# Eight PSUM banks as a ring of pairs and a ring of single banks, and a new order of fc1, fc2 and the chunks' bursts

## The chip, the cores and the metric

The kernel runs on one core of one Trainium2 chip. The metric is the device time of one execution in microseconds; the kernel before takes 4109.72 us (median of three runs, 4108.55 to 4111.58). Five engines work beside each other: TensorE (PE; its weight loads are shown apart as PEld), VectorE (DVE), ScalarE (ACT), GpSimd (POOL) and SyncE (SP), which here only starts transfers. Matmuls write to PSUM, which has 8 banks of 512 fp32 values in each of 128 partitions. A bank can be written again only when ACT or DVE has read ("evicted") what is in it.

## What is computed

The reference normalizes an image of 8 channels, sends it through a small Fourier network and adds the result to the image; then it adds a 3 x 3 dilation of the normalized sum. There are 8 images of 256 x 256. Cut to what matters:

```python
x = x + fno(gn(x))                      # 8 images, 4 groups of 2 channels
x = x + dilate_3x3(gn(x))               # max over 3x3, border -2

def fno(x):                             # each group has WID = 10 channels inside
    h = gconv1x1(concat(x, grid), fc0)
    for i in range(4):                  # the four "layers"
        h1 = irfft2(mix(rfft2(h)))      # 24 x 12 modes are mixed, the rest is zero
        h2 = gconv1x1(h, w[i])
        h = h1 + h2
        if i < 3: h = gswish(h, beta[i])
    h = gswish(gconv1x1(h, fc1), beta[3])   # 10 -> 128 channels in each group
    return gconv1x1(h, fc2)                 # 128 -> 2
```

All arithmetic is fp32.

## The kernel before

An image's rows lie in 11 chunks. For each layer the kernel computes, chunk by chunk:

- the **burst** (tile `p_z`): h1 + h2 of a chunk in four banks, 16 small matmuls for the 1x1 convolution (32 x 32 tiles of the PE array) and 8 for the inverse transform along a row (32 x 128 tiles); ACT evicts it with Silu;
- the **turn**: DVE transposes the chunk's new h in blocks of 32 x 32 into one of three slots of `turned`;
- for each two chunks the **transform** along the row (`p_d`, four banks) and the **gather** (`p_u`, one bank), whose copy is what the next layer's spectrum reads.

Between layers come the spectrum across the rows (`p_at`, `p_b`), the mixing of modes on DVE (`mix`, `p_f`) and the tables for the next bursts (`p_g`). The last two convolutions of an image, its **head**, are 128 steps: **fc1** (`p_fc` at L627, four banks, 32 x 128 tiles, ACT evicts with Silu) and, for every two steps, **fc2** (`p_fc` at L649, one bank, 128 x 32 tiles, DVE adds it to y). The head of image b is interleaved with the layers of image b + 1, and the dilation of the image before with both, as generators that are stepped:

```python
def ps_z(name):                                    # all of PSUM: four pairs of banks
    return ps.tile([128, 2, 512], F32, tag="z", bufs=4, name=name)
def ps_a(name):
    return ps_z(name)[:, 0, :]

def copy(i, dst, src):                             # alone: no head runs (image 0)
    if alone[0] and i % 2: nc.scalar.activation(dst, src, AF.Identity)
    else:                  nc.vector.tensor_copy(dst, src)
def copy_2(i, dst, src):
    if i % 2: nc.scalar.activation(dst, src, AF.Identity)      # L199
    else:     nc.vector.tensor_copy(dst, src)                  # L201

# spectrum across the rows: eight transposes into a pair
    t = ps_z(f"p_at_{b}_{l}_{j0}")                             # L320, copied at L195
# tables for the bursts, two channels in a pair
    p = ps_z(f"p_g_{b}_{l}_{o}")                               # L404 / L409, copied at L195
# ... (cut)

def turn(c):                                                   # L430, two DVE transposes
    ...
def transform(k):
    pair = [ps_z(f"p_d_{b}_{l}_{k}_{i}") for i in range(2)]
    for v in range(8):
        for q in range(NQ):
            mm(pair[q // 2][part(v % 4), q % 2, : 240 * n], fw8[part(q), v, :], t[...], ...)   # L447
    for i in range(2):
        copy_2(i, e[:, 2 * i : 2 * i + 2], pair[i][:, :, : 240 * n])
def gather(k):
    p = ps_a(f"p_u_{b}_{l}_{k}")
    ...                                                        # L461, copied at L464 / L467
def burst(c):
    pair = [ps_z(f"p_z_{b}_{l}_{c}_{i}") for i in range(2)]
    ...                                                        # L476 / L479, then L482
    for i in range(2):
        dst = h[:, c, 2 * i : 2 * i + 2, :]
        if l < 3: nc.scalar.activation(dst, pair[i], AF.Silu)                  # L488
        else:     nc.scalar.activation(dst, pair[i], AF.Identity, bias=bias3)  # L490

# one layer; "yield (n,)" asks for exactly n head steps, a plain number for a share of them,
# "even" / "odd" for one step more if the count of steps is not so
        if l == 3:
            yield "odd"
            for c in range(NCH):
                burst(c)
                ...                                # side work: the next image's first spectrum
                yield (LAST,)                      # LAST = 2
            return
        yield "even"
        for c in range(NCH):
            k = c // 2
            if c % 2 == 0:
                burst(c)
                yield (1,)
                turn(c)
                if k > 0: transform(k - 1)
            else:
                burst(c)
                if k > 0: gather(k - 1)
                yield (1,)
                turn(c)
        out_["sw"] = [load_sw(l + 1, 0), load_sw(l + 1, 1)]
        yield 1
        gather(k - 1)
        transform(k)
        yield 2
        gather(k)
        yield 1

# the head
        def first(n):
            pair = [ps_z(f"p_fc1_{b}_{n}_{i}") for i in range(2)]
            for g in range(G):
                mm(pair[g // 2][:, g % 2, :], w1[part(g), blk, :], hs[k][part(g), :], ...)     # L627
            for i in range(2):
                nc.scalar.activation(act[:, 2 * i : 2 * i + 2, :], pair[i], AF.Silu)           # L629
        def second(n):
            y, acc = box["y"], ps_a(f"p_fc2_{b}_{n}")
            ...                                                # L649: steps n and n + 1; added at L654
        for n in range(STEPS):
            if n % 2 == 0 and n > 3: second(n - 4)
            first(n)
            yield
        second(STEPS - 4)
        second(STEPS - 2)
```

PE, DVE and ACT each run their instructions in the order in which they are written here. A tile of a tag takes the place of the tile of that tag that many allocations (`bufs`) earlier, and waits for its last reader.

Of the kernel before, what the change touches and what calls it, by code (L numbers as in the profile page):

```python
# [10 lines left out]
F32 = mybir.dt.float32  # L11
AF = mybir.ActivationFunctionType
# [6 lines left out]
HW = 256  # L19
# [13 lines left out]
NBLK = 3  # L33
NCH = 11
NQ = 4
CS = 2 * NCH
PIX = 2 * HW
DR = 2
STEPS = 128
LAST = 2  # L40
SIDE = 4.2


# [1 line left out]
def fno_dilate_kernel(ctx: ExitStack, tc: tile.TileContext, a: dict, out: bass.AP):  # L45
    nc = tc.nc
    mm = nc.tensor.matmul
# [4 lines left out]
    ps = ctx.enter_context(tc.tile_pool(name="ps", bufs=2, space=PSUM))  # L52
# [1 line left out]


    def ps_z(name):
        return ps.tile([128, 2, 512], F32, tag="z", bufs=4, name=name)

    def ps_a(name):
        return ps_z(name)[:, 0, :]  # L60

    def part(i):
        return slice(32 * i, 32 * i + 32)
# [23 lines left out]
    fw8 = load("fw8", (128, 8, 32), nc.sync)  # L87
# [14 lines left out]
    bias3 = load("bias3", (128, 1))  # L102
    w1 = load("w1", (128, NBLK, HID))
# [4 lines left out]
    h = const.tile([128, NCH, NQ, PIX], F32, tag="h", name="h")  # L108
# [82 lines left out]
    def copy(i, dst, src):  # L191
        if alone[0] and i % 2:
            nc.scalar.activation(dst, src, AF.Identity)  # L193
        else:
            nc.vector.tensor_copy(dst, src)  # L195

    def copy_2(i, dst, src):
        if i % 2:
            nc.scalar.activation(dst, src, AF.Identity)  # L199
        else:  # L200
            nc.vector.tensor_copy(dst, src)  # L201
# [23 lines left out]
    def spectrum_x(b, out_):  # L225
# [19 lines left out]
        for half in range(2):  # L245
            xn = x[:, half].rearrange("p (r w) -> p r w", r=8)
            for r in range(0, 8, 4):
                t = ps_z(f"p_xt_{b}_{half}_{r}")
                for i in range(8):
                    nc.tensor.transpose(  # L250
                        t[:, i // 4, 128 * (i % 4) : 128 * (i % 4 + 1)],
                        xn[:, r + i // 2, 128 * (i % 2) : 128 * (i % 2 + 1)], ident,
                    )
                dst = xt[half][:, :, r : r + 4, :].rearrange("p f (u r) c -> p u r f c", u=2)
                src = t.rearrange("p u (r f c) -> p u r f c", r=2, f=2)
                for u in range(2):
                    copy(u, dst[:, u], src[:, u])
                yield 1.4
        yield 2
        p = ps_a(f"p_a0_{b}")  # L260
# [136 lines left out]
    def rows_of(b, l):  # L397

        zv = zt[:, :, :, : NBLK * WID].rearrange("p r f (n o) -> p o n r f", n=NBLK)
        for o in range(0, WID, 2):  # L400
            p = ps_z(f"p_g_{b}_{l}_{o}")
            for u in range(2):
                if l % 2 == 0:
                    mm(p[:, u, : NBLK * CS * NQ], fz[:, o + u].rearrange("p g k -> p (g k)"),  # L404
                       rowg.rearrange("p n j r -> p (n j r)"), start=True, stop=True)
                else:
                    for g in range(G):
                        for j in range(NQ):
                            mm(p[part(j), u, NBLK * CS * g : NBLK * CS * (g + 1)], fz[:, o + u, g, :],  # L409
                               rowg[:, :, j, :], start=True, stop=True)  # L410
            for u in range(2):
                src = p[:, u, : NBLK * CS * NQ]
                if l % 2 == 0:
                    dst = zv[:, o + u].rearrange("p n r f -> p n f r")
                    src = src.rearrange("p (n f r) -> p n f r", n=NBLK, r=CS)
                else:
                    dst = zv[:, o + u].rearrange("p n r f -> p f n r")
                    src = src.rearrange("p (f n r) -> p f n r", f=NQ, n=NBLK)
                copy(u, dst, src)
            yield 0.7  # L420


    def layer(b, l, out_, stored, side):
        group_in_f = l % 2 == 1

        def turn(c):

            dst = turned[:, c % 3].rearrange("p (s f x) -> p f s x", s=2, f=NQ)
            for i in range(2):
                nc.vector.transpose(  # L430
                    dst[:, 2 * i : 2 * i + 2], h[:, c, 2 * i : 2 * i + 2].rearrange("p f (s x) -> p f s x", s=2))
# [5 lines left out]
        def transform(k):  # L437


            cs = chunks_of(k)  # L440
            n, lo = len(cs), cs[0] % 3
            step = cs[-1] % 3 - lo if n == 2 else 1
            t = turned[:, lo : lo + step * (n - 1) + 1 : step].rearrange("p n (r v i) -> p n r v i", r=2 * NQ, v=8)
            pair = [ps_z(f"p_d_{b}_{l}_{k}_{i}") for i in range(2)]
            for v in range(8):
                for q in range(NQ):
                    mm(pair[q // 2][part(v % 4), q % 2, : 240 * n], fw8[part(q), v, :],  # L447
                       t[part(q), :, :, v, : NBLK * WID], start=v < 4, stop=v >= 4)
            e = turned[:, (2 * k + 1) % 3, : 960 * n].rearrange("p (q x) -> p q x", q=NQ)
            for i in range(2):  # L450
                copy_2(i, e[:, 2 * i : 2 * i + 2], pair[i][:, :, : 240 * n])

        def gather(k):

# [12 lines left out]
                    nc.vector.tensor_copy(zt[:, 2 * c : 2 * c + 2, :, : NBLK * WID], src[:, 2 * i : 2 * i + 2])  # L467

        def burst(c):
            pair = [ps_z(f"p_z_{b}_{l}_{c}_{i}") for i in range(2)]  # L470
            for f in range(NQ):
                for q in range(NQ):
                    o = pair[q // 2][part(f), q % 2, :]
                    if l == 0:
                        k = slice(32 * q, 32 * q + 6)
                        mm(o, wcn[k, :], h[k, c, f, :], start=True, stop=False)  # L476
                    else:
                        g = f if group_in_f else q
                        mm(o, wt[part(q), l, g, :], h[part(q), c, f, :], start=True, stop=False)  # L479
            for s in range(2):  # L480
                for q in range(NQ):
                    mm(pair[q // 2][:, q % 2, HW * s : HW * (s + 1)],  # L482
                       zt[part(q), 2 * c + s].rearrange("p f o -> p (f o)"), binv[part(q), :],
                       start=False, stop=s == 1)
            for i in range(2):
                dst = h[:, c, 2 * i : 2 * i + 2, :]
                if l < 3:
                    nc.scalar.activation(dst, pair[i], AF.Silu)  # L488
                else:
                    nc.scalar.activation(dst, pair[i], AF.Identity, bias=bias3)  # L490
            if l == 3:
                nc.sync.dma_start(stored[c], h[:, c].rearrange("p f w -> p (f w)"))

# [5 lines left out]
        if l == 0:  # L499
            for c in range(NCH):  # L500
                read_x(c)
            wcn = sb.tile([128, 32], F32, tag="wcn", bufs=1, name=f"wcn_{b}")
            nc.vector.tensor_scalar(wcn, wc, out_["mr"][:, 1:2], None, ALU.mult)
        if l == 3:
            room = 0.0
            yield "odd"
            for c in range(NCH):
                burst(c)
                room += SIDE
                while room > 0.0:  # L510
                    room -= next(side, SIDE)
                yield (LAST,)
            return
        yield "even"
        for c in range(NCH):
            k = c // 2
            if c % 2 == 0:
                burst(c)
                yield (1,)
                turn(c)  # L520
                if k > 0:
                    transform(k - 1)
            else:
                burst(c)
                if k > 0:
                    gather(k - 1)
                yield (1,)
                turn(c)
        out_["sw"] = [load_sw(l + 1, 0), load_sw(l + 1, 1)]
        yield 1  # L530
        gather(k - 1)
        transform(k)
        yield 2
        gather(k)
# [72 lines left out]
    def head(b, stored, stats):  # L607
# [13 lines left out]
        def first(n):  # L621

            k, blk = n // 32 * NCH + n % 32 // NBLK, n % 32 % NBLK
            act = sb.tile([128, G, 512], F32, tag="act", bufs=4, name=f"act_{b}_{n}")
            pair = [ps_z(f"p_fc1_{b}_{n}_{i}") for i in range(2)]
            for g in range(G):
                mm(pair[g // 2][:, g % 2, :], w1[part(g), blk, :], hs[k][part(g), :], start=True, stop=True)  # L627
            for i in range(2):
                nc.scalar.activation(act[:, 2 * i : 2 * i + 2, :], pair[i], AF.Silu)  # L629
            acts[n] = act  # L630

        def second(n):
# [34 lines left out]
        for n in range(STEPS):  # L667
            if n % 32 % NBLK == 0:
                load_state(n // 32 * NCH + n % 32 // NBLK + 2)
            if n % 2 == 0 and n > 3:  # L670
                second(n - 4)
            first(n)
            yield
        second(STEPS - 4)
        second(STEPS - 2)


# [243 lines left out]
```

## Time and profile before

| | kernel before |
|---|---|
| time, median of 3 | 4109.72 us |
| span in the profile | 4109.4 us |
| PE / PEld busy | 93% / 37% |
| ACT / DVE busy | 70% / 60% |
| mean granted clock of PE | 0.979 |
| image 0 without a head | about 365 us from the start |
| layers 0, 1, 2 of image 2 with a head | 78.6, 75.4, 76.8 us |
| layer 3 of image 2 with a head | 86.6 us |
| the last head alone, after layer 3 of image 7 | about 275 us |

The first four rows are on the page of the profile; the clock comes from the view of the cores; the stages are read from the timeline, from the first burst of a layer to the first matmul of the stage that follows it. A busy PE is not a PE at its peak: matmuls overlap in the pipeline and their ends are modelled, so the time that a group of matmuls costs is better read from its start to the start of the next group. "Idle before" in a group's line names what ended the wait; an engine that is not the bottleneck loses nothing by waiting.

### The profile page before, as it was taken

How to read it: one execution, taken by the hardware profiler on the slowest of the kernel's cores; microseconds unless marked ns; L12 is line 12 of the kernel's file. 1: busy time of each engine (PE TensorE's matmuls, PEld its weight loads, DVE VectorE, ACT ScalarE, POOL GpSimd, SP SyncE). 2: the span in 40 equal slices, each digit the busy share in tenths (PEclk: the TensorE clock that was granted, in tenths of full speed). 3: DMA queues.
4: the chain of work that ended last, by engine and by line, in shares of the span. 5: the costliest groups of instructions: out<-in, count | busy, mean ns of one | idle time of the engine just before them, and what ended most of it. 6: DMA issues, size and time to landing. Idle time of an engine off the chain costs nothing. (4 is left out here: it accounts for less than half of the span.)

```text
span 4109.4 us, 120095 instructions
## 1 busy us (share of the span) xinstructions
PE 3822.8 (93%) x54250; PEld 1529.8 (37%) x54250; DVE 2472.1 (60%) x3529; ACT 2860.1 (70%) x2997; POOL 117.0 (3%) x202
## 2 busy tenths in 40 slices
PE   5768999999999999999999999999999999999997
PEld 2434433333333343433333334343433433333222
DVE  6665565556566566665666666655676666663533
ACT  3436676776767777676777766777676776668887
POOL 1000000000000000000000000000000000000000
PEclk8988999999999999999999999999999999999998
DMA  2014111422125211261113511144121531215311
GB/s 83 14 46 157 56 42 33 163 88 64 57 75 175 64 57 57 83 195 43 58 57 108 175 47 48 49 145 136 55 58 47 169 101 59 61 47 191 94 52 48
DMA packets 113991, 345.09 MB, mean 84 GB/s; under 512 B 15772, under 2 KB 18396, under 8 KB 98057
## 3 DMA queue, kind: packets, MB, share of 16 engines
q1 hardware_dynamic: 95288, 276.33, 21.5%
q0 software_dynamic: 18192, 61.08, 4.5%
q8 instruction: 427, 7.00, 0.7%
q14 instruction: 84, 0.68, 0.1%
HBM read 213.36 MB, written 123.74 MB: 82 GB/s over the span
## 5 line engine op out<-in xcount | busy, mean ns | idle before, releaser
L629 ACT ACTIVATE act<-p_fc 128x1024 f32<-128x1024 f32 x2048 | 1961.8, 1026 | 735.1 <-PE p_fc L627 730.8
L627 PE MATMUL p_fc<-hs,c_w 32*128 32x512 f32 x8192 | 1201.7, 632 | 14.6 <-issue 8.3
L649 PE MATMUL p_fc<-act,c_w 128*32 128x512 f32 x8192 | 996.9, 603 | 47.1 <-ACT act L629 35.5
L627 PEld LDWEIGHTS p_fc<-hs,c_w 32*128 32x128 f32 x8192 | 398.3, 183 | 690.0 <-ACT act L629 270.4
L488 ACT ACTIVATE h<-p_z 128x1024 f32<-128x1024 f32 x528 | 511.7, 1021 | 189.1 <-PE p_z L482 188.6
L430 DVE STREAM_TRANSPOSE turned<-h 128x1024 f32<-128x1024 f32 x528 | 622.9, 1219 | 20.2 <-ACT h L488 19.9
L654 DVE TENSOR_TENSOR y<-p_fc,y 128x512 f32<-128x512 f32 x392 | 271.0, 691 | 543.0 <-PE p_fc L649 541.6
L649 PEld LDWEIGHTS p_fc<-act,c_w 128*32 128x32 f32 x8192 | 222.1, 110 | 636.2 <-issue 349.3
L482 PE MATMUL p_z<-c_binv,zt 32*128 32x256 f32 x5632 | 411.1, 405 | 0.9 <-ACT zt L193 0.9
L479 PE MATMUL p_z<-h,c_wt 32*32 32x512 f32 x8448 | 371.3, 602 | 6.7 <-DVE y L652 3.8
L482 PEld LDWEIGHTS p_z<-c_binv,zt 32*128 32x128 f32 x5632 | 261.3, 186 | 306.2 <-issue 289.1
L447 PE MATMUL p_d<-turned,c_fw 32*32 32x480 f32 (+1 forms) x9216 | 310.6, 541 | 12.5 <-DVE turned L430 12.5
L195 DVE COPY zt<-p_g 128x264 f32<-128x264 f32 x300 | 162.4, 629 | 169.5 <-PE p_g L409 94.0
L490 ACT ACTIVATE h<-p_z,c_bias 128x1024 f32<-128x1024 f32 x176 | 186.5, 1110 | 48.1 <-PE p_z L482 47.8
L199 ACT ACTIVATE turned<-p_d 128x960 f32<-128x960 f32 x144 | 130.0, 903 | 97.4 <-PE p_d L447 97.4
L447 PEld LDWEIGHTS p_d<-turned,c_fw 32*32 32x32 f32 x9216 | 121.8, 103 | 188.9 <-issue 151.3
L362 DVE TENSOR_REDUCE S<-turned 128x80 f32<-128x800 f32 x192 | 188.9, 984 | 5.0
L359 DVE TENSOR_TENSOR turned<-t,B 128x800 f32<-128x800 f32 x192 | 188.5, 982 | 0.9 <-DMA t<-in_spw 0.9
L461 PE MATMUL p_u<-turned,c_stack 128*32 128x480 f32 (+1 forms) x1152 | 137.9, 548 | 45.1 <-DVE turned L201 43.0
L479 PEld LDWEIGHTS p_z<-h,c_wt 32*32 32x32 f32 x8448 | 94.3, 103 | 205.8 <-ACT act L629 68.3
L201 DVE COPY turned<-p_d 128x960 f32<-128x960 f32 x144 | 152.1, 1057 | 30.3 <-PE p_d L447 30.1
L195 DVE COPY turned<-p_at 88x1024 f32<-88x1024 f32 x90 | 101.7, 1155 | 75.8 <-PE p_at L320 70.7
(172 smaller groups left out, 2134.7 us busy)
## 6 DMA issues: line engine op xcount, KB each, us to landing
stored<-h SPq DMA_DIRECT2D x88, 1024.0 KB
hs<-stored SPq DMA_DIRECT2D x352, 256.0 KB
t<-in_spw SPq DMA_DIRECT2D x96, 400.0 KB
yin<-y_rows POOLq DMA_DIRECT2D x56, 512.0 KB, 4.8
h<-in_xp SPq DMA_DIRECT2D x352, 48.0 KB
turned<-in_x SPq DMA_DIRECT2D x16, 1024.0 KB
y<-in_x SPq DMA_DIRECT2D x56, 256.0 KB
y_rows<-y POOLq DMA_DIRECT2D x56, 256.0 KB, 2.3
```

Of the source, the lines that this page charges most:

```text
L195: nc.vector.tensor_copy(dst, src)
L359: nc.vector.tensor_tensor(pr, sw[k], bt[:, k2, k].unsqueeze(2).to_broadcast([128, G, 2 * WID, WID]), ALU.mult)
L362: nc.vector.tensor_reduce(s[k2][:, k].rearrange("p g s o -> p (g s o)"), pr.rearrange("p g m i -> p (g m) i"), AX.X, ALU.add,)
L430: nc.vector.transpose(dst[:, 2 * i : 2 * i + 2], h[:, c, 2 * i : 2 * i + 2].rearrange("p f (s x) -> p f s x", s=2))
L447: mm(pair[q // 2][part(v % 4), q % 2, : 240 * n], fw8[part(q), v, :], t[part(q), :, :, v, : NBLK * WID], start=v < 4, stop=v >= 4)
L479: mm(o, wt[part(q), l, g, :], h[part(q), c, f, :], start=True, stop=False)
L482: mm(pair[q // 2][:, q % 2, HW * s : HW * (s + 1)], zt[part(q), 2 * c + s].rearrange("p f o -> p (f o)"), binv[part(q), :], start=False, s ...
L488: nc.scalar.activation(dst, pair[i], AF.Silu)
L627: mm(pair[g // 2][:, g % 2, :], w1[part(g), blk, :], hs[k][part(g), :], start=True, stop=True)
L629: nc.scalar.activation(act[:, 2 * i : 2 * i + 2, :], pair[i], AF.Silu)
L649: mm(acc[part(g), :], w2[:, g, 15 - rb - i : 47 - rb - i], act[:, g, :], start=i == 0, stop=i == 1)
L654: nc.vector.tensor_tensor(y, sums, y, ALU.add)
```

## The change

PSUM becomes two rings: two pairs of banks, and four single banks. What needs four banks (burst, transform, fc1) takes a single, a pair and a single and is evicted in three parts; what needs one (fc2, gather and the small sums) takes a single and no longer occupies a pair. The tables and the first transposes of an image take two singles. The pair of a transform is copied by ACT and its two singles by DVE.

The order is new as well. Each burst of an even chunk stands between two fc1, so that its last matmuls are followed by matmuls in the same 32 x 128 shape. fc2 follows the odd step and takes the activations of the steps n - 3 and n - 2. Where a head runs, both turns of a pair of chunks come after the gather.

```diff
     def ps_z(name):
-        return ps.tile([128, 2, 512], F32, tag="z", bufs=4, name=name)
+        return ps.tile([128, 2, 512], F32, tag="z", bufs=2, name=name)
     def ps_a(name):
-        return ps_z(name)[:, 0, :]
+        return ps.tile([128, 512], F32, tag="a", bufs=4, name=name)
+    def ps_4(name):
+        a, p, b = ps_a(name + "_a"), ps_z(name + "_p"), ps_a(name + "_b")
+        parts = [(0, 1, a.unsqueeze(1)), (1, 2, p), (3, 1, b.unsqueeze(1))]
+        return [a, p[:, 0, :], p[:, 1, :], b], parts
 ... copy_2
-        if i % 2:
+        if i == 1:
 ... first transposes (p_xt) and tables (p_g)
-            p = ps_z(f"p_g_{b}_{l}_{o}")
+            p = [ps_a(f"p_g_{b}_{l}_{o}_{u}") for u in range(2)]
 ... transform; burst and first(n) alike
-            pair = [ps_z(f"p_d_{b}_{l}_{k}_{i}") for i in range(2)]
+            banks, parts = ps_4(f"p_d_{b}_{l}_{k}")
-            for i in range(2):
-                copy_2(i, e[:, 2 * i : 2 * i + 2], pair[i][:, :, : 240 * n])
+            for i, m, t in parts:
+                copy_2(i, e[:, i : i + m], t[:, :, : 240 * n])
 ... layer
+        yield "even"
         if l == 3:
-            yield "odd"
             for c in range(NCH):
+                yield (1,)
                 burst(c)
 ...
-                yield (LAST,)
+                yield (1,)
             return
-        yield "even"
-        for c in range(NCH):
+        for c in range(0, NCH, 2):
             k = c // 2
-            if c % 2 == 0:
-                burst(c)
-                yield (1,)
-                turn(c)
-                if k > 0:
-                    transform(k - 1)
-            else:
-                burst(c)
-                if k > 0:
-                    gather(k - 1)
-                yield (1,)
-                turn(c)
+            yield (1,)
+            burst(c)
+            yield (1,)
+            if k > 0:
+                transform(k - 1)
+            if alone[0]:
+                turn(c)
+            if c + 1 < NCH:
+                burst(c + 1)
+            if k > 0:
+                gather(k - 1)
+            for i in range(c + alone[0], min(c + 2, NCH)):
+                turn(i)
         out_["sw"] = [load_sw(l + 1, 0), load_sw(l + 1, 1)]
         yield 1
-        gather(k - 1)
         transform(k)
 ... head
-            if n % 2 == 0 and n > 3:
-                second(n - 4)
             first(n)
+            if n % 2 == 1 and n > 2:
+                second(n - 3)
             yield
-        second(STEPS - 4)
         second(STEPS - 2)
```

## The prediction

> **What bounds the kernel now.** I read the busy times first, then the groups, the waits, and last the timeline of single stages, because a mean over stages with different limits decides nothing here.
>
> ```profile
> PE 3822.8 (93%) x54250; PEld 1529.8 (37%) x54250; DVE 2472.1 (60%) x3529; ACT 2860.1 (70%) x2997; POOL 117.0 (3%) x202
> ...
> L629 ACT ACTIVATE act<-p_fc 128x1024 f32<-128x1024 f32 x2048 | 1961.8, 1026 | 735.1 <-PE p_fc L627 730.8
> L627 PE MATMUL p_fc<-hs,c_w 32*128 32x512 f32 x8192 | 1201.7, 632 | 14.6 <-issue 8.3
> ```
>
> TensorE (PE) is busy 93% of the span; ScalarE (ACT) waits for it in nearly all of its 735 idle microseconds before L629. So a change must shorten PE's own work or its waits for a PSUM bank. The waits view says that such waits exist and are short, each about a microsecond:
>
> ```profile
> PEld p_fc L627 <- ACT act L629: 270.4, 388, 1.7
> ...
> PEld p_fc L649 <- ACT act L629: 206.2, 295, 1.4
> ```
>
> How much PE time they cost is read from starts in the timeline. One cycle of layers 0 to 2 (two chunks and two head steps), PE alone; columns: start, length, engine, line, tiles.
>
> ```profile
> 1008.38 1.92 PE L649 MATMUL p_fc<-act,c_w 128*32 128x512 f32 x16
> 1010.23 1.14 PE L627 MATMUL p_fc<-hs,c_w 32*128 32x512 f32 x8
> 1011.30 2.19 PE L447 MATMUL p_d<-turned,c_fw 32*32 32x480 f32 x61
> 1012.93 0.59 PE L479 MATMUL p_z<-h,c_wt 32*32 32x512 f32 x1
> 1012.95 0.59 PE L447 MATMUL p_d<-turned,c_fw 32*32 32x480 f32 x3
> 1013.15 1.45 PE L479 MATMUL p_z<-h,c_wt 32*32 32x512 f32 x31
> 1014.53 1.15 PE L482 MATMUL p_z<-c_binv,zt 32*128 32x256 f32 x16
> 1015.86 1.01 PE L461 MATMUL p_u<-turned,c_stack 128*32 128x480 f32 x8 [0.18 <-DVE turned L201]
> 1016.80 1.14 PE L627 MATMUL p_fc<-hs,c_w 32*128 32x512 f32 x8
> 1017.87 1.18 PE L479 MATMUL p_z<-h,c_wt 32*32 32x512 f32 x32
> 1018.98 1.15 PE L482 MATMUL p_z<-c_binv,zt 32*128 32x256 f32 x16
> ```
>
> From start to start: fc2 (L649) 1.85 us, fc1 (L627) 1.07, transform (L447) 1.60, the burst's first part (L479) 1.10 and second part (L482) 1.08, gather (L461) 0.96. Two bursts, two fc1 and one of each of the others make 10.9. Four cycles, to the fc2 at 1055.30, take 11.73 each, so about 0.8 us of a cycle is waiting: the burst at 1012.93 gets its second pair only when the eviction of the fc1 ends (ACT, 1011.46 + 1.94 = 1013.40), and the gather waits for the DVE copy, as its line says.
>
> [...] the burst's second part takes 1.08 us up to an fc2 of another shape (1018.98 to 1020.06) but 0.97 up to an fc1 of the same 32x128 shape (830.93 to 831.90). [...] Here two evictions of 1024 end after 1.94 with 1.03 each, so they start 0.915 apart; 480 columns more cost 0.40 us (0.97 against 0.57 in the transform's ACT copies), so 1024 columns are 0.85 and the fixed part is 0.06. [...]
>
> **The change, part by part.**
>
> *Cycle of layers 0 to 2.* New PE order: fc1, burst, fc1, fc2, transform, burst, gather. One burst is now followed by fc1 (0.97 for 1.08), so the work is 10.8. Waits under the new rings (fc1, burst and transform each take bank, pair, bank; singles come back after four): let the odd chunk's L482 start at 0. ACT takes its three parts from 1.18 to 3.17 (0.49 + 0.915 + 0.58 for the last), and a PE load restarts about 0.19 after such an end (836.06 to 836.25 in layer 3), so 3.36. The next burst needs this last bank first, and PE would be there at 1.08 + 0.96 + 1.07 = 3.11: wait 0.25. The fc1 after it is held by about 0.05, fc2, transform and the second burst find their banks free. DVE in a cycle: two turns 4.74, two copies of 480 1.2, gather copy 0.7, sum 0.7, dilation up to 2.6, within 11 us but late by some tenths in one cycle of three: 0.1. The cycle is 10.8 + 0.25 + 0.1 = 11.15, a gain of 0.58. Full cycles: 4 in a layer, 21 layers with a head (7 images x 3): 84 x 0.58 = 49; the first and last chunks perhaps 0.4 a layer, 8. **Together -57 us.**
>
> *The layer's end.* The instruction order of the changed kernel shows DVE turning chunk 10 after the copy of the fourth gather, where before it turned it ahead of the copies of the fourth transform. The same stretch of the kernel before, PE and then DVE:
>
> ```profile
> 933.45 2.24 PE L447 MATMUL p_d<-turned,c_fw 32*32 32x480 f32 x64
> 937.03 1.01 PE L461 MATMUL p_u<-turned,c_stack 128*32 128x480 f32 x8 [1.34 <-DVE turned L201]
> 937.98 1.44 PE L447 MATMUL p_d<-turned,c_fw 32*32 32x240 f32 x64
> ```
> ```profile
> 933.13 2.36 DVE L430 STREAM_TRANSPOSE turned<-h 128x1024 f32<-128x1024 f32 x2
> 935.73 1.16 DVE L201 COPY turned<-p_d 128x960 f32<-128x960 f32 x1 [0.24 <-PE p_d L447]
> 938.11 0.72 DVE L467 COPY zt<-p_u 128x240 f32<-128x240 f32 x2 [1.22 <-PE p_u L461]
> ```
>
> Before, the last transform follows the gather after 0.95. Afterwards it must wait for gather end (1.08 after its start) + copy 0.72 + turn 2.37 + handovers 0.15 = 4.3, so PE stands still 3.4 us, with nothing between in layers 0 and 2. In layer 1 one fc1 fills a microsecond, but the same fc1 used to fill the 1.34 ahead of the gather. 21 x 3.4: **+71 us.**
>
> *Rows (L404, L409).* fc1 takes two of four singles, each pair of tables two. In "fc1, table, fc1" the second fc1's last bank is the first fc1's last bank, evicted at 1.24 + 1.89 + 0.1 = 3.2 us after its start, where PE arrives at 2.1: one wait of 1.1. Placed in the four orders of rows of an image, such waits and shorter ones (0.35 to 0.9) make about 9 us an image against some 3 before (layer 1: PE work 16.8, measured 17.7). 6 x 7: **+41.**
>
> *Inverse spectrum (L320).* Its tiles stay pairs but find two in place of four, and share them with fc1; a copy takes 1.2. Some 0.8 a stage, 21 stages: **+17.**
>
> *Layer 3.* Order unchanged (burst, fc1, fc2, fc1). Its period of 6.39 (829.86 to 836.25) is a loop: L479 1.07, L482 to ACT 1.18, burst eviction 2.01 until fc1's eviction, that one 1.94, restart 0.19. The loop stays, since the burst's first bank is again fc1's last, and each eviction gets one instruction more: 0.06 and, with a bias, about 0.1. 77 chunks x 0.16 = 13, and some 5 for the side work's transposes, now two singles each: **+18.**
>
> *Mixing and the last head.* Before, the round of fc1, fc1, fc2 takes 4.165: ACT starts 1.24 after fc1, its first 1024 columns need 1.03, fc2 waits for that pair and takes 1.85 (with 0.04 to restart). Now the first bank is free after 0.6, and the next limit is the second fc1, waiting for the eviction of the previous one: about 4.08. 0.08 x (66 + 84): **-12.**
>
> *Image 0, no head.* DVE now copies twice, turns, and only then copies the gather; a pair of chunks takes about 8.85 for 8.4, 15 pairs, and the spectrum loses a little: **+10.**
>
> Sum: -57 + 71 + 41 + 17 + 18 - 12 + 10 = +88. The terms for rows, spectrum and image 0 count waits that I placed by hand, and PE may make some of them good where ACT and DVE catch up in a stop; I take off about 20: **4175 us, +1.6%.**
>
> **The rivals.** (a) *The cycle wins.* If all waits in it vanish, the gain is 0.9 x 84 + 15 = 90, with -12 for the head; if rows and spectrum cost nothing, the layer's end still takes 71: about 4080. For it speaks that PE is 93% busy and that fc1 and burst share a shape; against it that the profile shows only 0.11 us for such a switch and that the turn's place is certain. (b) *ACT becomes the bound.* 2048 + 704 evictions of 1024, two to a set, become three to a set: 1376 more instructions x 0.06 = 83 us of ACT time. In a cycle ACT has 4 x 1.89 + 0.97 = 8.5 of 11 us, so it is not the bound there; in layer 3 (5.9 of 6.4) and in mixing (3.8 of 4.1) it nearly is. If a short eviction starts 0.6 and not 0.49 after the one before it, the two lengthen by 0.2 to 0.5 a round: 4230. (c) *DVE becomes the bound of the cycle*, as dilation and turns stand ahead of the transform's copies: 0.5 a cycle more, 4215.
>
> **Range and chances.** The layer's end is the surest term (within 10 us); the cycle is uncertain by 25, rows and spectrum by 30, layer 3 by 15; together some 45. Range 4090 to 4240. 2% lies at 4192 and 4028: slower by more is two in five, faster by more needs every loss but the layer's end to vanish and more.
>
> **What would show it.** In the changed profile: cycles of 11.0 to 11.3 us; a wait of the transform's load for the turn, some 21 times and over 2 us, near 65 us in total; layer 3's period at 6.5 to 6.6; waits of fc1 for its own eviction in the rows; the head's round near 4.08. I am wrong if the transform has no such wait, if rows take no longer than before, or if the cycle falls below 10.9 or stays above 11.5.

## The result, and the profile after

The changed kernel takes 4224.6 us (median of four runs, 4218.59 to 4229.15), the kernel before 4109.2: a ratio of 1.028, interval 1.0261 to 1.0297. It is slower by 115 us. The prediction said 4175, with a range up to 4240. The direction and several single terms were right, but the middle was 50 us too low.

The first page of the profile after, and three rows of its view of waits (who waited for whom: us in total, times, longest):

```profile
PE 3872.9 (92%) x54250; PEld 1563.8 (37%) x54250; DVE 2474.6 (59%) x3673; ACT 2933.6 (69%) x4373; POOL 119.8 (3%) x202
```
```profile
PEld p_fc_a L631 <- ACT act L633: 256.6, 341, 1.1
...
PE p_d_a L451 <- DVE turned L434: 83.1, 39, 3.2
...
PEld p_fc_b L631 <- ACT act L633: 55.5, 78, 1.6
```

ACT has 1376 instructions more (4373 against 2997) and is busy 73 us longer, but its share falls: it is not the bound. The transform (`p_d_a`) now waits for the turn, up to 3.2 us at a time (before at most 1.4, 12.5 in all). fc1 waited for its own eviction before too (270.4 us); now it does so at its first bank and, for 55.5 us, again at its last (`p_fc_b`).

The busy sums don't say where 115 us went, so I cut the span at the first matmul of each stage. Head steps are spread differently in the kernels, so each number is the stage's time less 1.07 us for every fc1 and 1.85 for every fc2 in it (their lengths from start to start). The table shows the difference from the kernel before, in us of one profiled execution; the experiments below are in it already. "Mixing and rows" is `p_f` and `p_g`; layer 3 is that of images 1 to 6.

| stage | before | changed | e3_rings | e4_order | e5_fill | e10_singles | e7_before_fill |
|---|---|---|---|---|---|---|---|
| image 0, no head | 308 | +16 | +9 | +15 | +21 | +13 | +2 |
| spectrum (`p_at`, `p_b`) | 180 | +13 | +9 | +4 | +22 | +28 | 0 |
| mixing and rows | 197 | +52 | +52 | +26 | +58 | +4 | +1 |
| layers 0 to 2 | 999 | +43 | 0 | +82 | -39 | -44 | -26 |
| layer 3 | 249 | +1 | +12 | -7 | +1 | -10 | -1 |
| layer 3 of image 7, last head | 76 | -8 | -5 | -2 | -8 | -7 | -1 |

The changed column adds up to 117. Two stages hold 95 of it: the layers, and the rows between them. The row of image 0 is the least certain: the changed kernel, e5_fill, e6_last and e9_warm run the same instructions there, and show +16, +21, +15 and +23.

**The end of a layer.** DVE at the end of layer 0 of image 2 (start, length, engine, line, tiles), the first matmul of the last transform, then two stretches of the same place with the busy time of PE, PEld, DVE, ACT and POOL, the granted clock and DMA:

```profile
972.36 0.66 DVE L206 COPY turned<-p_d_a 128x480 f32<-128x480 f32 x1 [0.34 <-PE p_d_b L451]
972.93 0.65 DVE L206 COPY turned<-p_d_b 128x480 f32<-128x480 f32 x1
974.80 0.72 DVE L471 COPY zt<-p_u 128x240 f32<-128x240 f32 x2 [1.22 <-PE p_u L465]
975.44 2.36 DVE L434 STREAM_TRANSPOSE turned<-h 128x1024 f32<-128x1024 f32 x2
```
```profile
977.94 0.38 PE L451 MATMUL p_d_a<-turned,c_fw 32*32 32x240 f32 x1 [3.20 <-DVE turned L434]
```
```profile
973.00:978.00 5.00, 1.07 (x16) 0.28 (x22) 3.58 (x6) 0.33 (x1) 0.00 (x0) 1.00 0.00 0
978.00:981.40 3.40, 3.40 (x72) 1.80 (x76) 0.72 (x2) 0.57 (x1) 0.00 (x0) 0.52 0.00 0
```

This is the predicted picture: the gather's copy, behind it the turn of the last chunk, and the transform can start only at 977.94. DVE took the turn in the written order: ACT had ended the eviction of that chunk at 969.41 (968.81 + 0.60), yet the turn started at 975.44, behind the gather's copy, for which DVE itself had waited 1.22 us. PE works 1.07 of the 5 us. What I had not foreseen is in the second stretch. PE comes back at half its clock (0.52 granted over 3.40 us). Such stretches go with the stops only in part. With each of the 14 stops of 3.2 us (layers 0 and 2 of seven images) comes a stretch at half the clock, begun late in the stop or just behind it, of 3.4 us ten times and of 6.8 us four times, 61 us together. But five stretches of 10.2 us and one of 6.8 begin 8 to 13 us into a layer 0; of the 3.41 us just before, PE had been busy for all ahead of the five, and for 2.51 ahead of the one. After 390 us all stretches, with one of 23.9 us at the very end, add up to 147 us, against 75 in the kernel before.

**The rows.** Weight loads in the rows of layer 1 of image 2:

```profile
1027.56 0.18 PEld L631 LDWEIGHTS p_fc_a<-hs,c_w 32*128 32x128 f32 x1
...
1028.65 0.29 PEld L631 LDWEIGHTS p_fc_b<-hs,c_w 32*128 32x128 f32 x2 [0.78 <-ACT act L633]
1029.70 0.16 PEld L653 LDWEIGHTS p_fc<-act,c_w 128*32 128x32 f32 x8 [0.76 <-issue]
```

The second fc1 starts at 1027.56, but its last bank can be loaded only at 1028.65, when ACT has emptied that bank; the fc1 takes 2.14 us for its 1.07.

**The cycle.** From gather to gather the median is 11.43 us, before it was 11.69. The gain is 0.26 and not the 0.58 of the prediction.

### The profile page after: what moved, and what is told of

It is laid out like the page before. It is cut to its first block, busy times and chain, and to the rows that moved or that the text cites. A ratio compares the mean times of both kernels' runs of the same rounds, so it can differ in the third digit from the quotient of the medians.

```text
span 4225.7 us, 120734 instructions
## 1 busy us (share of the span) xinstructions
PE 3872.9 (92%) x54250; PEld 1563.8 (37%) x54250; DVE 2474.6 (59%) x3673; ACT 2933.6 (69%) x4373; POOL 119.8 (3%) x202
## 5 line engine op out<-in xcount | busy, mean ns | idle before, releaser
L631 PE MATMUL p_fc_b<-hs,c_w 32*128 32x512 f32 x2048 | 1133.2, 641 | 7.2 <-ACT act L633 2.7
L631 PE MATMUL p_fc_a<-hs,c_w 32*128 32x512 f32 x2048 | 1118.6, 636 | 14.4 <-ACT act L633 12.2
L631 PE MATMUL p_fc_p<-hs,c_w 32*128 32x512 f32 x4096 | 1124.5, 636 | 0.0
L633 ACT ACTIVATE act<-p_fc_p 128x1024 f32<-128x1024 f32 x1024 | 1062.0, 1037 | 0.5
L633 ACT ACTIVATE act<-p_fc_a 128x512 f32<-128x512 f32 x1024 | 622.8, 608 | 603.7 <-PE p_fc_b L631 482.3
L633 ACT ACTIVATE act<-p_fc_b 128x512 f32<-128x512 f32 x1024 | 636.9, 622 | 1.2 <-PE p_fc_b L631 1.2
L486 PE MATMUL p_z_p<-c_binv,zt 32*128 32x256 f32 x2816 | 405.1, 406 | 0.0
L486 PE MATMUL p_z_a<-c_binv,zt 32*128 32x256 f32 x1408 | 402.6, 405 | 0.0
L486 PE MATMUL p_z_b<-c_binv,zt 32*128 32x256 f32 x1408 | 402.5, 406 | 0.0
L451 PE MATMUL p_d_a<-turned,c_fw 32*32 32x480 f32 (+1 forms) x2304 | 309.0, 562 | 83.1 <-DVE turned L434 83.1
L483 PE MATMUL p_z_a<-h,c_wt 32*32 32x512 f32 x2112 | 347.0, 600 | 17.4 <-ACT act L633 14.1
L631 PEld LDWEIGHTS p_fc_b<-hs,c_w 32*128 32x128 f32 x2048 | 316.6, 187 | 74.3 <-ACT act L633 55.5
```

The costliest lines, as they stand in the source:

```text
L451: mm(banks[q][part(v % 4), : 240 * n], fw8[part(q), v, :], t[part(q), :, :, v, : NBLK * WID], start=v < 4, stop=v >= 4)
L486: mm(banks[q][:, HW * s : HW * (s + 1)], zt[part(q), 2 * c + s].rearrange("p f o -> p (f o)"), binv[part(q), :], start=False, stop=s == 1)
L631: mm(banks[g], w1[part(g), blk, :], hs[k][part(g), :], start=True, stop=True)
L633: nc.scalar.activation(act[:, i : i + m, :], t, AF.Silu)
```

## Experiments

All times of a run are compared with the kernel before on the same chip (4106 to 4109 us). None of the kernels leaves out a part of the computation.

### First set: which part costs what

**e1_turn**, the changed kernel with the last turn of a layer moved ahead:

```diff
+            if c + 1 == NCH:
+                turn(c)
             if k > 0:
                 transform(k - 1)
 ... and it is left out of the turns after the gather
```

> The changed kernel with one thing moved: the turn of the last chunk (c = 10) stands ahead of the fourth transform again. Theory (the turn's place in DVE's queue stops PE at each layer's end, 14 x 3.2 + 7 x 2.1 us in the changed profile): the wait of the last transform for the turn is gone and the time falls by 55 to 62, to about 4165. Rival (PE's stop lets ACT and DVE catch up, and it is the three-part evictions that cost): less than 15 of it comes back, 4210 or more.

Measured: 4212.9 us, ratio 1.026 (1.0245 to 1.0276). A miss: 12 us gained, not 55 to 62. DVE at the end of the same layer, and PE's gather:

```profile
953.39 2.36 DVE L434 STREAM_TRANSPOSE turned<-h 128x1024 f32<-128x1024 f32 x2
955.68 0.62 DVE L206 COPY turned<-p_d_a 128x480 f32<-128x480 f32 x1
956.22 0.64 DVE L206 COPY turned<-p_d_b 128x480 f32<-128x480 f32 x1
958.89 0.72 DVE L471 COPY zt<-p_u 128x240 f32<-128x240 f32 x2 [2.03 <-PE p_u L465]
...
957.00 1.83 PE L465 MATMUL p_u<-turned,c_stack 128*32 128x480 f32 x8 [3.25 <-DVE turned L206]
```

The turn now stands ahead of the transform's copies, and the gather waits 3.25 us for them. PE stops as long as before, one step earlier, and the half-clock stretches stay (157 us). So DVE is behind here with whatever is queued: of the two places tried, the turn's place in the queue decides which wait is the long one, not whether there is one. The number is the rival's, but not its cause: with the old evictions the order loses even more in the layers (e4_order, below).

**e2_tables**, the changed kernel with the tables in a pair:

```diff
-            p = [ps_a(f"p_g_{b}_{l}_{o}_{u}") for u in range(2)]
+            pair = ps_z(f"p_g_{b}_{l}_{o}")
+            p = [pair[:, u, :] for u in range(2)]
```

> The changed kernel with one thing undone: the tables for the bursts (p_g) take a pair again, out of the ring of two pairs, so that fc1, table, fc1 no longer meet in the ring of four singles. Theory (the rows stage lost 7 to 8 us an image to the ring of singles): the rows gain 35 to 50 us over the seven images with a head, 4175 to 4190. Rival (the stage is bound by ACT's longer sets of three evictions): under 15 us, 4210 or more.

Measured: 4232.1 us, ratio 1.0303 (1.0286 to 1.032); again a miss. The rows get about 13 us shorter in the whole run. fc1's wait at its last bank falls from 55.5 to 21.8 us, but now the tables themselves stand, as the view of waits has it:

```profile
PEld p_g L414 <- PE p_fc_b L632: 23.9, 21, 1.4
```

The view names fc1; but in layer 1 of image 2 such a table is loaded at 1030.59, just after DVE has copied the table before it (1030.48), whose place in the ring it takes. So a good part of the wait has only moved to the ring of pairs. The layers, image 0 and the last head take 5, 6 and 5 us longer, with more half-clock stretches (171 us in all), which eats up the rest.

**e3_rings**, the old order on the new rings, and **e4_order**, the new order on the four old pairs, each take one half of the change's diff:

```diff
 e3_rings: kernel before
+    pairs bufs=2, singles bufs=4, ps_4; three evictions; tables and first transposes in two singles
 e4_order: changed kernel
-    pairs bufs=2, singles bufs=4, ps_4; three evictions; tables and first transposes in two singles
+    ps.tile([128, 2, 512], F32, tag="z", bufs=4); two evictions of 1024; as before
```

> The kernel before, in its old order, with the new rings and the three-part evictions alone. Theory: no stop at the layer's end, but the rows (some 40 to 50), the spectrum (10) and image 0 (a few) lose, and the cycle and the head gain a little: 4145 to 4175. Rival 1 (the three-part evictions carry the whole loss): 4210 or more. Rival 2 (the order carries the whole loss): about 4110.

> The new order alone: PSUM stays four pairs, evictions stay 1024 wide. Theory: the stop at the layer's end costs its 60, the cycle gives some 25 back through the fc1 next to the burst, image 0 loses some 10 for its order: 4145 to 4165. Rival 1 (evictions carry the loss): at or under 4110. Rival 2 (the order carries the whole loss): 4210 or more.

Measured: e3_rings 4185.8 us, ratio 1.0188 (1.0172 to 1.0205); e4_order 4215.6, ratio 1.027 (1.0248 to 1.0293). Both are slower than I had expected, and e4's number is that of its second rival (the order carries the whole loss), which e3's own loss refutes. Each part alone is a loss, of 79 and 109 us, and together they lose 115. The table says how that fits: the rings lose in the rows (+52) and nothing in the layers; the order loses in the layers (+82) and half as much as the rings in the rows (+26). On the old pairs the new order doesn't shorten the cycle at all (11.72 us); only with the rings does it (11.43), so in the layers the rings give back about 40 of what the order costs.

### Second set: the end of a layer

**e5_fill** and **e6_last** are the changed kernel, **e8_order_fill** is e4_order, **e7_before_fill** is the kernel before, with one edit each:

```diff
 e5_fill, and e8_order_fill alike: two head steps between the fourth gather and the last transform
-        yield 1
+        yield (2,)
         transform(k)
 e6_last: the last chunk's turn between the transform's copies and the gather
-            if alone[0]:
+            if alone[0] or c + 1 == NCH:
                 turn(c)
 ... and the turns after the gather begin one later
 e7_before_fill: one head step, always, ahead of the fourth gather
-        yield 1
+        yield (1,)
         gather(k - 1)
```

> The changed kernel, with exactly two head steps (fc1, fc1, fc2) between the fourth gather and the last transform where it had a share of them that came to none in layers 0 and 2. Theory (the stop of the transform at the end of a layer, 59.6 us, and the half-clock stretches that follow it, up to 36 us, are lost time): the head's work fills the stop, the waits of L451 for the turn fall under 15 us in total, the half-clock stretches fall back to about 75 us, and the time is about 4140 us (4125 to 4160). Rival (the head's work is a fixed sum and only moves from layer 3 or the last head; DVE is behind by the same amount and stops PE elsewhere): over 4200 us.

> The changed kernel, with the turn of the last chunk of a layer put after the copies of the fourth transform and ahead of the fourth gather. Theory (the last transform stands because this turn is queued behind the gather's copy): its wait falls from 3.2 us to about 1.2, the half-clock stretches are fewer, 4170 to 4185 us. Rival (DVE is behind at the end of a layer whatever the place, as when the turn stood ahead of the transform's copies): the gather waits for what the transform no longer does, 4205 to 4225 us.

> The kernel before, with exactly one head step ahead of the fourth gather at the end of a layer, so that an fc1 always stands between the fourth transform and that gather. Theory (a stop of PE is lost time wherever the head could have filled it): the gather's waits of 1.3 us in layer 0 and 2.4 us in layer 2 go, and perhaps some of the half-clock stretches with them: 4075 to 4095 us. Rival (the head's steps only move): 4105 to 4115 us.

> The new order on the four old pairs (evictions of 1024), with two head steps between the fourth gather and the last transform. Theory (of the 109 us that the new order costs on the old pairs, the layers' ends and the clock after them are about 80): 4130 to 4150 us. Rival (the order's loss lies in the cycles, where fc1 and burst wait for pairs): over 4190 us.

| run | time, us | ratio to before (interval) | against its parent |
|---|---|---|---|
| e5_fill | 4162.1 | 1.0125 (1.0108 to 1.0142) | -62.5 (changed kernel) |
| e6_last | 4180.7 | 1.0172 (1.0157 to 1.0187) | -44 (changed kernel) |
| e8_order_fill | 4149.0 | 1.0094 (1.0079 to 1.0109) | -67 (e4_order) |
| e7_before_fill | 4081.1 | 0.9927 (0.9909 to 0.9945) | -28 (before) |

e6_last, e7 and e8 came out as the theory said. In e6 the transform's wait is 1.26 us in layers 0 and 2 and 0.3 in layer 1, 19.8 us with a head in place of 59.6; and the head's work fills a stop in each of the three places where it was put into one. e5_fill won about 62 where I expected some 85. Two rows of its view of waits tell why:

```profile
PE p_d_a L451 <- DVE turned L434: 23.1, 18, 1.8
...
PE p_f L382 <- DVE F L374: 68.8, 25, 12.7
```

The transform's wait has gone from 83.1 to 23.1, and what is left lies in image 0. But the mixing's matmul (`p_f`) now waits 68.8 us for DVE, in the changed kernel 53.6. The layers have 21 fc1 more (315 for 294), and just these are missing in the spectrum (217 for 238), at whose end they used to cover DVE's mixing of modes. In the table the layers gain 82 against the changed kernel: the 59.6 us of the wait, and 22 of the half clock behind it (see e9_warm). Spectrum, rows and image 0 lose 20, of which the 5 of image 0, where no head runs, do not come from the edit. e7_before_fill takes its steps from the rows instead, which get shorter by just these steps (178 fc1 for 192, and +1 in the table): it loses nothing, and is the fastest kernel of this study, with neither part of the change in it.

### Third set: the clock, the rows, and one more idea

**e9_warm**, the changed kernel with idle matmuls in the stop, to part the low clock from the wait:

```diff
         yield 1
+        if not alone[0]:
+            banks, _ = ps_4(f"p_warm_{b}_{l}")
+            for i in range(2):
+                for o in banks:
+                    nc.tensor.matmul(o[:, :HW], ident, binv, start=True, stop=True)
         transform(k)
```

> The changed kernel with eight idle matmuls (128 x 128 by 256 columns, their sums are read by nobody) ahead of the last transform of a layer with a head. They fill about 1.9 of the 3.2 us in which PE stands, and shorten no wait: the transform still starts when the turn is done. Theory (the half-clock stretches after the stop cost time of their own, beside the stop): the stretches after 390 us fall from 147 us to 75 to 95, and the time to 4185 to 4200 us. Rival (the low clock costs nothing, since PE would wait for ACT or DVE anyway): the stretches fall, and the time stays at 4218 to 4232 us.

Measured: 4222.3 us, ratio 1.0276 (1.0259 to 1.0294): the time of the changed kernel. The half-clock stretches fell from 147 to 55 us, so the numbers are the rival's. But the unchanged time is a gain and two losses. The eight matmuls took 3.7 us, not the 1.9 of my estimate: in the trace the transform starts 4.59 us after the gather in layers 0 and 2, in the changed kernel 4.21, and 6.12 against 4.65 in layer 1. 14 x 0.38 + 7 x 1.47 is 15.6 us of new stop. And image 0, with the same instructions, took 7 us longer in this execution. The gain is in what follows the stop: from the last transform to the last gather, layers 0 and 2 take 5.04 us in all 14 places, in the changed kernel 6.27 to 7.91, which makes 22 us.

e6_last shows the same within one kernel. These two stretches go from the last transform to the last gather of layer 2 in images 2 and 3, with the same 96 matmuls in each:

```profile
1227.30:1233.67 6.38, 6.38 (x96) 2.56 (x100) 1.19 (x4) 3.02 (x6) 0.00 (x0) 0.74 0.01 4
1730.28:1735.31 5.03, 5.03 (x96) 2.20 (x100) 1.19 (x4) 3.02 (x6) 0.00 (x0) 1.00 0.09 32
```

A mean clock of 0.74 over 6.38 us is 3.3 us at half the clock, and they cost 1.35 us, 0.4 of their length. Image 0 says as much: its layer 0 takes 53.9 us in the changed kernel and in e6_last, with 3.4 us at half the clock, and 60.9 and 61.4 in e5_fill and e9_warm, with 20.5 and 22.4. So the rival is wrong: the half clock costs time of its own, at the ends of layers 0 and 2 about 20 of the 115 us (the 22, less some 2 that the kernel before loses there).

**e10_singles**, e5_fill with the singles taken and evicted first:

```diff
-        a, p, b = ps_a(name + "_a"), ps_z(name + "_p"), ps_a(name + "_b")
-        parts = [(0, 1, a.unsqueeze(1)), (1, 2, p), (3, 1, b.unsqueeze(1))]
-        return [a, p[:, 0, :], p[:, 1, :], b], parts
+        a, b, p = ps_a(name + "_a"), ps_a(name + "_b"), ps_z(name + "_p")
+        parts = [(0, 1, a.unsqueeze(1)), (1, 1, b.unsqueeze(1)), (2, 2, p)]
+        return [a, b, p[:, 0, :], p[:, 1, :]], parts
 ... copy_2: ACT copies the pair
-        if i == 1:
+        if i == 2:
```

> e5_fill with one thing more: what takes four banks takes its two single banks first and its pair last, so ACT evicts the two singles first (after about 0.6 and 1.1 us in place of 0.6 and 1.9). Theory (the rows lose time because the second fc1's last single bank is evicted last): the second fc1 of the rows is no longer held by about 1 us, the rows lose some 35 of their 44 us, the cycles a few tenths: 4100 to 4130 us. Rival (in the rows ACT's sum of evictions is the limit, whatever their order): 4150 to 4165 us.

Measured: 4099.2 us, ratio 0.9974 (0.9964 to 0.9984). That is 63 us less than e5_fill, just below the range that I had given, and below the kernel before. Weight loads in the same rows as above:

```profile
998.28 0.29 PEld L631 LDWEIGHTS p_fc_a<-hs,c_w 32*128 32x128 f32 x2
998.45 0.18 PEld L631 LDWEIGHTS p_fc_b<-hs,c_w 32*128 32x128 f32 x1
...
999.52 0.16 PEld L653 LDWEIGHTS p_fc<-act,c_w 128*32 128x32 f32 x8 [0.76 <-DVE zt L200]
```

The second single is loaded 0.17 us after the first, where it was 1.09; fc1 takes 1.24 us, where it was 2.14. In the table mixing and rows fall from +58 to +4. So nearly the whole loss of the rows was one thing: the ring's next bank was the one that ACT emptied last. ACT's sum of evictions, the rival, has not changed (busy 2935.0 us, in e5_fill 2935.5).

**e11_old_order_singles** is e3_rings with the edits of e10_singles and e7_before_fill; **e12_gather_later** is e7_before_fill with

```diff
                 burst(c)
+                yield (1,)
                 if k > 0:
                     gather(k - 1)
-                yield (1,)
                 turn(c)
```

> The old order on the new rings (e3_rings), with the two singles taken and evicted first, and with the one head step ahead of the fourth gather of e7_before_fill. Theory: e3_rings was 79 us above the kernel before, the singles' order takes back 35 to 45 of it in the rows, the head step 25 to 30: 4105 to 4125 us. Rival (the rings' loss has another cause than the last single): 4150 to 4165 us. Above the kernel before with the same head step (4081 us) in either case.

> e7_before_fill with the gather of an odd chunk after the fc1 and not ahead of it, so that PE has work while DVE still copies the transform for it. Theory: the gather's remaining waits (about 20 us between 390 and 3800 us) go: 4058 to 4070 us. Rival (the gather's copy now stands later in DVE's queue and holds the turn and the next transform): 4080 to 4095 us.

Measured: e11 4092.7 us, ratio 0.996 (0.9945 to 0.9975), faster than the range that I had given. As on the new order, the singles' order takes most of the rings' loss away: it and the head step are worth 93 us together. It beats the kernel before, but not e7_before_fill (4081.1), which has the same order and the old pairs.

e12: 4142.0 us, ratio 1.0076 (1.0061 to 1.0091); 61 us slower than its parent where I expected a gain. Its cycle is 12.39 us, in e7 11.66: 0.73 x 84 cycles = 61. PE in layer 1 of image 2:

```profile
1041.52 1.04 PE L627 MATMUL p_fc<-hs,c_w 32*128 32x512 f32 x8
1042.81 1.01 PE L461 MATMUL p_u<-turned,c_stack 128*32 128x480 f32 x8 [0.25 <-ACT h L488]
1043.75 2.03 PE L479 MATMUL p_z<-h,c_wt 32*32 32x512 f32 x32
1045.71 1.15 PE L482 MATMUL p_z<-c_binv,zt 32*128 32x256 f32 x16
```

Nor is it my rival, DVE's queue. The gather now takes its pair after fc1, which makes that pair the one the burst just filled: it waits for ACT (`h L488`), and the next burst gets a pair that fc1 has only just written (1.96 us to the next group's start, where 1.11 is usual). Two allocations have changed places, and with them the banks that every later tile of the cycle waits for.

## Why the prediction was right or wrong

The range held and the direction was right. By its own terms, with the table's numbers:

- **The cycle: wrong size, the largest error.** I gave 0.58 a cycle, 49 us, and 8 for first and last chunks. Measured: 0.26, or 22 us. The step that failed is the reading "the burst at 1012.93 gets its second pair only when the eviction of the fc1 ends". From transform to the burst's second part that took 3.23 us, where 1.60 and 1.10 make 2.70, and I took the half microsecond for a wait. PE of the kernel before in image 0, where there is no fc1 at all:

```profile
169.19 2.19 PE L447 MATMUL p_d<-turned,c_fw 32*32 32x480 f32 x61 [0.68 <-DVE turned L430]
...
172.42 1.15 PE L482 MATMUL p_z<-c_binv,zt 32*128 32x256 f32 x16
```

  It is 3.23 there too, though the pair had been emptied (170.49) before the burst began (170.83), and 3.23 in the changed kernel:

```profile
1078.04 0.58 PE L451 MATMUL p_d_a<-turned,c_fw 32*32 32x480 f32 x1
...
1081.27 0.48 PE L486 MATMUL p_z_a<-c_binv,zt 32*128 32x256 f32 x1
```

  So it is PE's own time, and the end of the eviction at 1013.40 only happened to fall into it. The work of a cycle is then 11.3 and not 10.8, and of 11.73 at most 0.4 could be won, not 0.58. A second error hides part of the first: of the 0.35 us of new waits that I counted, only about 0.1 came (11.43 less 11.33). Image 0 was in the profile and would have told me.
- **The layer's end: right, but without the half clock.** Predicted 21 stops of 3.4 us more, and a view of waits with about 65 us of them. Measured with a head: 14 of 3.2 and 7 of 2.11, 59.6 us. e6 shows that the time is really lost there: its layers are 47 us shorter, 40 of them wait and some 7 half clock. The half clock after the stops, 22 us, stood nowhere in the prediction. My reason, the turn's place, was only half: e1_turn shows that DVE's backlog stops PE ahead of the transform's copies too.
- **Rows: right in kind.** Predicted 41; e3_rings, with the same head steps, shows 52 for mixing and rows, and e10 shows the cause to be the one named (the first fc1's last bank, evicted last), though not each of its microseconds: in e10 two things are bettered at once, the bank's order and the cycles beside it.
- **Spectrum: right,** 17 predicted, 13 measured (9 with the rings alone).
- **Layer 3: wrong, by a compensation.** The rings alone cost 12 (predicted 18), though in another way: the plain period is 6.46 (0.07 more, not 0.16), and chunks with side work take 9.21 for 8.45. "Order unchanged" overlooked the new order's other count of head steps and fc2's place behind the odd step; e4_order gains 7 there. Together +1.
- **Mixing and last head: right in part,** -8 in the last stage; a round takes 4.02 (predicted 4.08, before 4.165).
- **Image 0:** 10 predicted, 16 measured, and 15 to 23 in executions of the same instructions.
- **The 20 us taken off for catching up** did not come; the measured terms add up to the whole. Two sums were a little off besides: 6 x 7 is 42 and not 41, and 88 less 20 on 4109.7 is 4178 and not 4175.

Of the rivals, (a) named the right condition (rows and spectrum free of cost; e10 nearly gives the rows) but held the cycle's gain to be more than three times what it is. (b), ACT as the bound, is refuted as the main cause by e10, which has the same 1376 more instructions and runs faster than the kernel before; e11, which has them too, stays 12 us behind e7_before_fill, which has the old pairs. (c), DVE in the cycle, didn't show; DVE held PE up at the layer's end, and in the mixing (53.6 us at `p_f`).

So the change's two ideas lose for reasons that are not in the ideas: one turn that leaves PE with nothing to do at 21 layer ends, and a ring whose next bank is the last to be emptied. With both mended the new order is level with the kernel before, and the kernel before with one head step moved is still faster than both. What stays open: why the new order costs 26 us in the rows on the old pairs, why half-clock stretches begin in layer 0 without a stop, and why the spectrum keeps 28 us in e10, of which the missing head steps under the mixing are only a part.

## What to carry to other kernels

What counted here in a ring of PSUM banks was when the next one in line is emptied: let the parts that the next tile needs first be evicted first (e10_singles: an fc1 of the rows in 1.24 us for 2.14), and look at the ring again whenever two allocations change places. Fill a stop with work from a stage that doesn't need it (in e7_before_fill the rows), not from one where it hides another engine's work (in e5_fill the spectrum: `p_f` waits 68.8 us for DVE, in the changed kernel 53.6). And before a gap in the timeline is taken for a wait, look for the same sequence where the supposed cause is absent. An unchanged time can be a gain and a loss (e9_warm): compare the stretch itself, with and without the cause, before it is called free.

## What I had not expected of the hardware

- A transform (32 x 32 tiles, 480 columns) followed by a burst takes 3.23 us to the burst's second part, in the kernel before with a head (1011.30 to 1014.53) and in its image 0 without one (169.19 to 172.42). To the burst's first matmul it is 1.63 (1011.30 to 1012.93), and a burst behind an fc1 takes 1.11 to its second part (1017.87 to 1018.98).
- With each of 14 stops of PE of 3.2 us came 3.4 or 6.8 us at half the clock; in e6_last the same holds for eight of 14 stops of 1.26 us, and five stretches of 10.2 us in the changed kernel had no stop just before them (PE was busy for all of the 3.41 us ahead of each).
- The same 96 matmuls took 5.03 us at the full clock and 6.38 with 3.3 us at half of it (e6_last): 0.4 of a stretch's length was lost.
- Eight matmuls of 128 x 128 by 256 columns in fp32 took about 3.7 us, 0.46 each (e9_warm); I had expected half of that. The trace has them as sixteen records some 0.22 us apart, two for each matmul, as it has eight for the four matmuls of an fc1.
